# A hybrid block on one core: scan terms added by four on GpSimd, a column-split out-projection, earlier fetches of head sums

## The chip, the cores and the metric

The kernel runs on one core of a Trainium2 chip. The core has five engines with their own queues, each worked off in order: TensorE (PE in the profile, with its weight loads as PEld), VectorE (DVE), ScalarE (ACT), GpSimd (POOL) and SyncE (SP), which here only issues DMAs. The metric is device time in microseconds of one execution; smaller is better.

## The reference

The input is an image batch `x` of (4, 128, 64, 64) in float32. Layer 0 is a convolutional block with a selective scan in it, layer 1 is attention followed by a mixture of experts.

```python
# layer 0: x = x + conv_block(group_norm(x))
xn = ln(group_norm(x));  y = xn + fc2(gelu(ln(depthwise3x3(xn))))
chunks = ln(y) split into 4 groups of 32 channels          # 16 sequences of 4096 tokens
xin, z = split(chunks @ in_proj.T)                          # 64 inner channels each
xin = silu(causal_conv1d(xin, 4 taps))
dt, Bm, Cm = split(xin @ x_proj.T);  delta = softplus(dt @ dt_proj.T + b)
h_t = exp(delta_t * A) * h_{t-1} + delta_t * B_t * xin_t    # 16 states n per channel
y_t = sum over n of C_t[n] * h_t[n]  + D_skip * xin_t
m = (y * silu(z)) @ out_proj.T + skip * chunks
x = x + ln(xn + m) @ proj.T + b
# layer 1, tokens t of (4, 4096, 128)
t = t + softmax(q k^T / sqrt(128)) v @ W_proj               # 4 heads of 32
p = softmax(ln(t) @ router);  take the top 2 of 8 experts, renormalised
t = t + sum over the two of p_e * (ln(t) @ expert_e + b_e)
```

## The kernel before

All work is in one program whose order on every engine is written out by hand: each instruction is issued through a small wrapper (`queued`, line 445) that chains it to the one before it on its engine. That is why almost every instruction carries line 445 in the profile, and why one goes by the names of tiles.

An image is cut into eight blocks of 512 tokens (`BLK`), which gives 32 blocks. The scan of a block is done in two halves `p` (64 of the 128 channels each, two chunks of 32) and for 16 states `n`, so 1024 units of one scan each. A loop over `slot` does one unit per turn, and beside it one group of attention, and stages of two lanes of other tasks. One slot holds, in this order:

- the DMAs that were collected by `send` go out on SP (`flush`), and SP fetches the rows of B and C of the unit three slots ahead (tile `rows`);
- ScalarE copies the last state and computes the decay `da` of the next unit;
- a group of attention: TensorE makes scores `sc` of two key tiles for 1024 queries from `qs` and `ks`, ScalarE takes their exp (`pT`);
- the unit's scan on VectorE (`scan`): the product `h` of the B row and `du`, the scan over 512 tokens into `h`, the product `hc` of the C row and `h`;
- stages of the lanes X and Y, a generator's step at a time (`advance`);
- TensorE sums `hc` over the states into the PSUM tile `y`, by a product with the identity; the term of a unit is due some slots after its scan (`due`);
- the weighted sums `av` of the attention group of the slot before (`weighted`).

For image 0 each `hc` is a product of its own, one slot after its scan. For the other images GpSimd adds the `hc` of an odd state onto that of the even state before it, and the sum is one product two slots later. `hc` has five buffers.

Lane Y runs the norms (`first_norm`), the convolution (`conv`: on TensorE for image 0, on VectorE for the others) and `inputs`, which makes `xin`, the gate `zs`, `delta`, `du` (on GpSimd) and the rows of B and C, which go to DRAM by way of the tile `bc`. Lane X runs `closed` for a block whose two scans are done: it multiplies the gated `y` (`zs`) by `wout`, two accumulated products of 128 columns into one PSUM tile; `wout[:, p]` has values only in the 64 output columns of half `p`. It goes on to the norm, the projection and the queries, keys and values. Keys and queries are kept as a high half `hi` (rounded to fp32r) and a low half `lo`, both sent to DRAM. ScalarE copies the PSUM tile to `full` and to `hi`, and one stage later VectorE subtracts them in `lower`. Lane X also runs `divided`, once for 1024 queries, which brings the attention sums of the four heads back from DRAM (tile `avl`, two buffers), transposes them on TensorE and divides by the denominators (`rden`, `ao`); and `finished`, which applies the router and the eight experts to a block.

Each lane has one PSUM tile at a time (`ps_X`, `ps_Y`), so the next product of a lane waits until the last one has been read. Attention of an image can begin once its first quarters are closed, and after the last scan some 157 groups of attention are left.

A second program part (`any_scores`) handles inputs with too large scores; it is not entered with these inputs.

Of the kernel before, what the change touches and what calls it, by code (L numbers as in the profile page):

```python
# [9 lines left out]
F32 = mybir.dt.float32  # L10
# [26 lines left out]
def conv_mamba_attn_moe_kernel(ctx: ExitStack, tc: tile.TileContext, t: dict):  # L37
# [637 lines left out]
    def inputs(b, i, p):  # L675

        xn, pairs = xn_of[b, i], pairs_of[b, i]
        r = slice(DI * p, DI * p + DI)
        ps = work("Y")
        summed(ps, [(inxc[:, j, :], pairs[:, p, 2 * j : 2 * j + BLK]) for j in range(2)])  # L680
        pz = work("X")
        mm(pz, inz[r, :], xn[r, 3 : 3 + BLK])
        yield
        xin = mix.tile([P, BLK], F32, name="xin", bufs=2)
        scalar.activation(xin, ps, AF.Silu, bias=cb)
        zs = mix.tile([P, BLK], F32, name="zs", bufs=4)
        scalar.activation(zs, pz, AF.Silu)
        yield

        pb = work("X")  # L690
        mm(pb[0:DI, :], wbc, xin)
        ps = work("Y")
        mm(ps, wdt, xin)
        yield
        bc = mix.tile([DI, BLK], F32, name="bc")
        scalar.copy(bc, pb[0:DI, :])
        bcd = dram.tile([2, NST, 2 * BLK], F32, name="bcd", bufs=4)
        send(bcd.rearrange("c n (k q) -> (c n k) q", k=2), bc)

        e = tmp("Y", "e")  # L700
        scalar.activation(e, ps, AF.Abs, bias=dtb)
        scalar.activation(e, e, AF.Exp, scale=-1.0)
        ln = tmp("Y", "ln")
        scalar.activation(ln, e, AF.Ln, bias=1.0)
        delta = mix.tile([P, BLK], F32, name="delta", bufs=2)
        scalar.activation(delta, ps, AF.Relu, bias=dtb)
        yield
        yield

        du = mix.tile([P, BLK], F32, name="du", bufs=2)  # L710
        lost = du
        gpsimd.tensor_scalar(lost, e, 1.0, -1.0, ALU.add, ALU.add)
        gpsimd.tensor_sub(lost, e, lost)
        gpsimd.tensor_add(ln, ln, lost)
        gpsimd.tensor_add(delta, delta, ln)
        gpsimd.tensor_mul(du, delta, xin)
        in_of[b, i, p] = xin, zs, delta, du, bcd
        yield
        yield
        yield  # L720
# [18 lines left out]
    def scan(b, i, p, n, w, da):  # L739

        du = in_of[b, i, p][3]
        h = mix.tile([P, BLK], F32, name="h", bufs=3)
        vector.tensor_mul(h, w[:, 0, :], du)
        vector.tensor_tensor_scan(
            out=h, data0=da, data1=h, initial=0.0 if i == 0 else states[b % 2][:, p, n : n + 1],
            op0=ALU.mult, op1=ALU.add,
        )
        hc = mix.tile([P, BLK], F32, name="hc", bufs=5)
        vector.tensor_mul(hc, w[:, 1, :], h)
        return h, hc  # L750

# [9 lines left out]
    def closed(b, i):  # L761

        if i == 0:
            kqv[b] = [], [], [], dram.tile([P, NTILE * C], F32, name="td")
        kd, qd, vd, td = kqv[b]
        j, u = divmod(i, 2)
        if u == 0:
            kd.append(dram.tile([P, 2, 2 * BLK], F32, name=f"kd{j}"))
            qd.append(dram.tile([P, 2, 2, 2 * BLK], F32, name=f"qd{j}"))
            vd.append(dram.tile([NH, 2, P, NT * 2 * DH], F32, name=f"vd{j}"))  # L770
        kd, qd, vd, sj = kd[j], qd[j], vd[j], slice(u * BLK, (u + 1) * BLK)
        s = slice(i * BLK, (i + 1) * BLK)
        cm = tmp("X", "cm")
        vector.scalar_tensor_tensor(
            cm.rearrange(IMAGE, w=IMG), xn_of[b, i][:, 3:].rearrange(IMAGE, w=IMG), skip,
            y0_rows(b, i), ALU.mult, ALU.add,
        )
        xr = load_x(t["xtok"][b], i, "xr")
        yield
        yield  # L780
        ps = work("X")
        summed(ps, [(wout[:, p, :], gated.pop((b, i, p))) for p in range(2)])
        yield
        vector.tensor_add(cm, ps, cm)
        gpsimd.tensor_add(by_tile(xr), by_tile(xr), projb[:, None, :].to_broadcast([P, NT, C]))
        yield
        ps = transposed("X", by_tile(cm))
        yield
        xt = yield from normalised("X", by_tile(ps))
        ps = transposed("X", xt)  # L790
        yield
        f = tmp("X", "f")
        scalar.activation(f, ps, AF.Identity, bias=lnb, scale=lnw)
        yield
        ps = work("X", [P, NT, C])
        for j in range(NT):
            mm(ps[:, j, :], f[:, j * P : (j + 1) * P], projT)
        yield
        tt = side.tile([P, NT, C], F32, name="tt")
        vector.tensor_add(tt, ps, by_tile(xr))  # L800
        send(tsave[b][:, s], tt.rearrange("p j c -> p (j c)"))
        xt = yield from normalised("X", tt)

        tr = tmp("X", "tr", [P, NT, C])
        gpsimd.tensor_add(tr, tt, crow[:, None, :].to_broadcast([P, NT, C]))
        send(td[:, s], tr.rearrange("p j c -> p (j c)"))
        ps = transposed("X", xt)
        yield
        xa = tmp("X", "xa")
        scalar.copy(xa, ps)  # L810
        yield
        split = []
        for d, w, bias in ((kd, wkn, bkn), (qd, wqn, bqn)):
            ps = work("X")
            mm(ps, w, xa)
            yield
            full = side.tile([P, BLK], F32, name="full")
            scalar.activation(full, ps, AF.Identity, bias=bias)
            hi = side.tile([P, BLK], F32R, name="hi", bufs=2)
            scalar.activation(hi, ps, AF.Identity, bias=bias)  # L820
            yield

            split.append((d, full, hi))
            lower(split.pop(), sj)
        ps = work("X", [P, NT, NH, DH])
        for j in range(NT):
            mm(ps[:, j].rearrange("p h d -> p (h d)"), xa[:, j * P : (j + 1) * P], wv)
        yield
        vector.tensor_copy(vst[:, :, :, 0:DH], ps.rearrange("p j h d -> p h j d"))
        send(vd[:, u].rearrange("h p q -> p h q"), vst.rearrange("p h j d -> p h (j d)"))  # L830
        yield
        yield
        yield

    def lower(what, s):
        d, full, hi = what
        lo = side.tile([P, BLK], F32R, name="lo", bufs=2)
        vector.tensor_sub(lo, full, hi.bitcast(F32))
        for half, w in enumerate((hi, lo)):
            w = w.bitcast(F32)  # L840
            if len(d.shape) == 4:
                send(d[:, :, half, s], w[:, None, :].to_broadcast([P, 2, BLK]))
            else:
                send(d[:, half, s], w)

# [124 lines left out]
    def divided(b, q):  # L972

        ao = att.tile([P, 2, NT, NH, DH], F32, name="ao", bufs=2)
        ao_of[b, q] = ao

        def load(h):
            w = att.tile([P, BLK], F32, name="avl", bufs=2)
            sync.dma_start(out=w, in_=partial.pop((b, q, h)))
            return w  # L980

        ahead = load(0)
        yield
        yield
        for h in range(NH):
            now = ahead
            if h + 1 < NH:
                ahead = load(h + 1)
            ps = transposed("X", by_tile(now))
            yield  # L990
            ps = ps.rearrange("p (j u d) -> p u j d", u=2, d=2 * DH)
            rden = small.tile([P, 2, NT, 1], F32, name="rden")
            vector.reciprocal(rden, ps[:, :, :, DH : DH + 1])
            vector.tensor_mul(
                ao[:, :, :, h, :], ps[:, :, :, 0:DH], rden.to_broadcast([P, 2, NT, DH])
            )
            yield
# [175 lines left out]

    groups = attention_groups()
    units = [(b, i, p, n) for b, i in blocks for p in range(2) for n in range(NST)]
    rows, decays, old, due = {}, {}, None, deque()
    even, y_of, waiting, slot = None, {}, None, 0
    while slot < len(units) or due or waiting or left or lanes["X"] or running:
        flush()

# [14 lines left out]
        if slot < len(units):  # L1195
            unit = units[slot]
            h, hc = scan(*unit, rows.pop(slot), decays.pop(slot))
            old = unit, h
            b, i, p, n = unit

            if b == 0:
                due.append((slot + 1, unit, hc, n == 0))
            elif n % 2 == 0:
                even = hc
            else:
                gpsimd.tensor_add(even, even, hc)
                due.append((slot + 2, unit, even, n == 1))
        if not taken:
            advance("X", True)

# [134 lines left out]
```

## Time and profile before

| | |
|---|---|
| median of 3 runs | 5853.91 us (5849.08 to 5866.08) |
| the profiled execution | 5853.82 us, span 5852.1 us |
| granted TensorE clock, mean | 0.94 |
| PE busy | 5075.6 us (87%) |
| DVE busy | 4221.9 us (72%) |
| ACT busy | 3988.0 us (68%) |
| POOL busy | 2033.6 us (35%) |
| DMA | 1030.33 MB, mean 176 GB/s |

The span is the time from the first to the last instruction of the program. Busy time is the union of an engine's instructions. Matmuls are pipelined and their ends are modelled, so what a matmul costs is better read from the starts of it and of the next one than from its duration. "Idle before" is the time an engine stood still before an instruction, and the name after the arrow is what ended the wait. float32 products are issued as two instructions each, the fp32r scores as one.

### The profile page before, as it was taken

The numbers are of one execution on the slowest core, as the hardware profiler recorded it, in microseconds if no ns is written. First come the engines' busy times: TensorE is split into PE (matmuls) and PEld (weight loads), VectorE is DVE, ScalarE is ACT, GpSimd is POOL, SyncE is SP. The second block draws the span as 40 slices with busy tenths as digits, with TensorE's granted clock in tenths as the row PEclk, the third lists the DMA queues.
The fourth block names the chain that finished last, engine by engine and source line by source line (L and its number), as shares of the span: only waits on it lengthen the run. The fifth ranks groups of instructions, "written<-read, shape, count | busy, mean of one in ns | idle before, by whom it ended". The sixth has DMA issues, their size and how long they took to land. (4 is left out here: it accounts for less than half of the span.)

```text
span 5852.1 us, 61426 instructions
## 1 busy us (share of the span) xinstructions
PE 5075.6 (87%) x18378; PEld 2129.7 (36%) x18378; DVE 4221.9 (72%) x7155; ACT 3988.0 (68%) x6116; POOL 2033.6 (35%) x1821
## 2 busy tenths in 40 slices
PE   4676898988989898898999998898999998998896
PEld 2222343333333333333333333333333343343332
DVE  4888766778877787787888887888888888712222
ACT  3454676877767776777777776677877777665452
POOL 2333222335423443444443443444443434310000
PEclk8777999999999998999999999999999999999997
DMA  3455565556545555556555555457555555533211
GB/s 98 167 177 169 196 203 182 190 209 223 202 149 172 198 186 197 172 198 219 185 199 199 188 199 191 155 196 252 191 192 199 183 201 185 190 134 102 99 58 35
DMA packets 405509, 1030.33 MB, mean 176 GB/s; under 512 B 42785, under 2 KB 126130, under 8 KB 405170
## 3 DMA queue, kind: packets, MB, share of 16 engines
q1 hardware_dynamic: 404002, 1025.53, 51.5%
q8 instruction: 149, 2.44, 0.2%
q14 instruction: 190, 1.56, 0.1%
q10 hardware_dynamic: 1168, 0.80, 0.1%
HBM read 875.11 MB, written 134.22 MB: 172 GB/s over the span
## 5 line engine op out<-in xcount | busy, mean ns | idle before, releaser
L445 ACT ACTIVATE pT<-sc 128x1024 f32<-128x1024 f32 x2048 | 1981.1, 1020 | 879.0 <-PE sc L445 875.5
L445 PE MATMUL av<-pT,v 128*64 128x512 f32 x8192 | 2012.4, 612 | 0.5 <-ACT avs L445 0.2
L445 DVE TENSOR_TENSOR_SCAN h<-da,state,h 128x512 f32<-128x512 f32 x896 | 1271.6, 1419 | 276.2 <-ACT da L445 191.5
L445 PE MATMUL sc<-qs,ks 128*128 128x512 f32 x4096 | 1326.7, 445 | 76.7 <-ACT pT L445 40.3
L445 POOL TENSOR_TENSOR hc<-hc 128x512 f32<-128x512 f32 x384 | 557.4, 1452 | 1541.4 <-DVE hc L445 1367.3
L445 PEld LDWEIGHTS sc<-qs,ks 128*128 128x128 f32 x4096 | 724.5, 193 | 663.0 <-issue 240.9
L445 PEld LDWEIGHTS av<-pT,v 128*64 128x64 f32 x8192 | 503.9, 138 | 1198.3 <-issue 1115.1
L445 DVE TENSOR_TENSOR hc<-rows,h 128x512 f32<-128x512 f32 x1024 | 828.2, 809 | 73.6 <-DVE h L445 2.3
L445 DVE TENSOR_TENSOR h<-rows,du 128x512 f32<-128x512 f32 x1024 | 821.7, 802 | 57.3 <-DMA rows<-bcd 30.9
L445 PE MATMUL y<-hc,ident 128*128 128x512 f32 x1280 | 734.3, 660 | 79.6 <-DVE hc L445 70.0
L445 ACT ACTIVATE da<-delta,amat 128x512 f32<-128x512 f32 x1024 | 749.7, 732 | 30.9 <-DVE h L445 28.7
L445 ACT COPY state<-h 128x1 f32<-128x1 f32 x896 | 176.8, 197 | 373.3 <-DVE h L445 373.0
L445 DVE SCALAR_TENSOR_TENSOR acc<-ps_X,prX,acc 128x128 f32<-128x128 f32 x864 | 301.8, 349 | 169.6 <-PE ps_X L445 145.3
L445 ACT ACT_TABLE_LOAD x318 | 408.0, 1283 | 20.0 <-PE ps_Y L445 15.3
L445 PE MATMUL ps_X<-w_ew,xf 128*128 128x512 f32 x432 | 257.2, 679 | 112.4 <-DVE acc L445 112.2
L445 PEld LDWEIGHTS y<-hc,ident 128*128 128x128 f32 x1280 | 248.7, 206 | 257.1 <-DVE hc L445 129.6
L445 DVE RECIPROCAL rden<-ps_X 128x8 f32<-128x8 f32 x64 | 13.0, 203 | 348.8 <-PE ps_X L445 348.6
L445 POOL TENSOR_SCALAR rsX<-mvX 128x4 f32<-128x4 f32 x92 | 48.3, 525 | 600.6 <-DVE mvX L445 593.6
L445 POOL TENSOR_SCALAR du<-e 128x512 f32<-128x512 f32 x64 | 129.3, 2020 | 322.3 <-ACT e L445 322.3
L445 POOL TENSOR_TENSOR avs<-avs,prev 128x512 f32<-128x512 f32 x64 | 94.6, 1478 | 420.4 <-ACT avs L445 345.8
L445 POOL TENSOR_SCALAR rsY<-mvY 128x4 f32<-128x4 f32 x100 | 54.9, 549 | 533.6 <-DVE mvY L445 532.0
L445 ACT ACTIVATE xt<-ps_Y,shiftY,rsY 128x128 f32<-128x128 f32 x380 | 143.5, 467 | 127.4 <-POOL shiftY L445 119.9
(244 smaller groups left out, 5052.1 us busy)
## 6 DMA issues: line engine op xcount, KB each, us to landing
rows<-bcd SPq DMA_DIRECT2D x1024, 512.0 KB, 4.9
ks<-kd SPq DMA_DIRECT2D x256, 512.0 KB, 6.3
qs<-qd SPq DMA_DIRECT2D x130, 512.0 KB, 5.6
v<-vd SPq DMA_DIRECT2D x256, 256.0 KB, 6.2
avd<-avs SPq DMA_DIRECT2D x128, 256.0 KB, 2.0
pairs<-xn SPq DMA_DIRECT2D x128, 128.5 KB, 2.4
qd<-hi SPq DMA_DIRECT2D x32, 512.0 KB, 5.6
qd<-lo SPq DMA_DIRECT2D x32, 512.0 KB, 5.9
```

The costliest lines, as they stand in the source:

```text
L445: return lambda *args, **kw: queued(op(*args, **kw))
```

## The change

It has four parts, and two changes of buffers that go with them. GpSimd adds four terms `hc` of successive states into one, and TensorE multiplies only the sum of four by the identity; terms are left alone in the first half of image 0 (slots 0 to 127, `ALONE`) and no longer in its second half; `hc` has six buffers. The out-projection writes two separate products of 64 columns into the two halves of the PSUM tile. The head sums are fetched two heads ahead, with three buffers. The low half is computed by VectorE from the PSUM tile in one operation, right after `hi`, and `full` and `lower` go. The tile `bc` takes its place in the rotation of lane Y's four scratch buffers.

```diff
--- before.py
+++ after.py
@@ -692,7 +692,7 @@
         ps = work("Y")
         mm(ps, wdt, xin)
         yield
-        bc = mix.tile([DI, BLK], F32, name="bc")
+        bc = tmp("Y", "bc")[0:DI, :]
         scalar.copy(bc, pb[0:DI, :])
         bcd = dram.tile([2, NST, 2 * BLK], F32, name="bcd", bufs=4)
         send(bcd.rearrange("c n (k q) -> (c n k) q", k=2), bc)
@@ -745,7 +745,7 @@
             out=h, data0=da, data1=h, initial=0.0 if i == 0 else states[b % 2][:, p, n : n + 1],
             op0=ALU.mult, op1=ALU.add,
         )
-        hc = mix.tile([P, BLK], F32, name="hc", bufs=5)
+        hc = mix.tile([P, BLK], F32, name="hc", bufs=6)
         vector.tensor_mul(hc, w[:, 1, :], h)
         return h, hc
 
@@ -779,7 +779,9 @@
         yield
         yield
         ps = work("X")
-        summed(ps, [(wout[:, p, :], gated.pop((b, i, p))) for p in range(2)])
+        for p in range(2):
+            r = slice(DI * p, DI * p + DI)
+            mm(ps[r, :], wout[:, p, r], gated.pop((b, i, p)))
         yield
         vector.tensor_add(cm, ps, cm)
         gpsimd.tensor_add(by_tile(xr), by_tile(xr), projb[:, None, :].to_broadcast([P, NT, C]))
@@ -809,19 +811,23 @@
         xa = tmp("X", "xa")
         scalar.copy(xa, ps)
         yield
-        split = []
         for d, w, bias in ((kd, wkn, bkn), (qd, wqn, bqn)):
             ps = work("X")
             mm(ps, w, xa)
             yield
-            full = side.tile([P, BLK], F32, name="full")
-            scalar.activation(full, ps, AF.Identity, bias=bias)
             hi = side.tile([P, BLK], F32R, name="hi", bufs=2)
             scalar.activation(hi, ps, AF.Identity, bias=bias)
+            lo = side.tile([P, BLK], F32R, name="lo", bufs=2)
+            vector.scalar_tensor_tensor(
+                lo, ps, bias, hi.bitcast(F32), ALU.add, ALU.subtract
+            )
+            for half, w in enumerate((hi, lo)):
+                w = w.bitcast(F32)
+                if len(d.shape) == 4:
+                    send(d[:, :, half, sj], w[:, None, :].to_broadcast([P, 2, BLK]))
+                else:
+                    send(d[:, half, sj], w)
             yield
-
-            split.append((d, full, hi))
-            lower(split.pop(), sj)
         ps = work("X", [P, NT, NH, DH])
         for j in range(NT):
             mm(ps[:, j].rearrange("p h d -> p (h d)"), xa[:, j * P : (j + 1) * P], wv)
@@ -831,17 +837,6 @@
         yield
         yield
         yield
-
-    def lower(what, s):
-        d, full, hi = what
-        lo = side.tile([P, BLK], F32R, name="lo", bufs=2)
-        vector.tensor_sub(lo, full, hi.bitcast(F32))
-        for half, w in enumerate((hi, lo)):
-            w = w.bitcast(F32)
-            if len(d.shape) == 4:
-                send(d[:, :, half, s], w[:, None, :].to_broadcast([P, 2, BLK]))
-            else:
-                send(d[:, half, s], w)
 
 
 
@@ -975,17 +970,17 @@
         ao_of[b, q] = ao
 
         def load(h):
-            w = att.tile([P, BLK], F32, name="avl", bufs=2)
+            w = att.tile([P, BLK], F32, name="avl", bufs=3)
             sync.dma_start(out=w, in_=partial.pop((b, q, h)))
             return w
 
-        ahead = load(0)
+        ahead = deque(load(h) for h in range(2))
         yield
         yield
         for h in range(NH):
-            now = ahead
-            if h + 1 < NH:
-                ahead = load(h + 1)
+            now = ahead.popleft()
+            if h + 2 < NH:
+                ahead.append(load(h + 2))
             ps = transposed("X", by_tile(now))
             yield
             ps = ps.rearrange("p (j u d) -> p u j d", u=2, d=2 * DH)
@@ -1173,8 +1168,10 @@
 
     groups = attention_groups()
     units = [(b, i, p, n) for b, i in blocks for p in range(2) for n in range(NST)]
+
+    ALONE = NB // 2 * 2 * NST
     rows, decays, old, due = {}, {}, None, deque()
-    even, y_of, waiting, slot = None, {}, None, 0
+    four, y_of, waiting, slot = None, {}, None, 0
     while slot < len(units) or due or waiting or left or lanes["X"] or running:
         flush()
 
@@ -1198,13 +1195,14 @@
             old = unit, h
             b, i, p, n = unit
 
-            if b == 0:
+            if slot < ALONE:
                 due.append((slot + 1, unit, hc, n == 0))
-            elif n % 2 == 0:
-                even = hc
+            elif n % 4 == 0:
+                four = hc
             else:
-                gpsimd.tensor_add(even, even, hc)
-                due.append((slot + 2, unit, even, n == 1))
+                gpsimd.tensor_add(four, four, hc)
+                if n % 4 == 3:
+                    due.append((slot + 2, unit, four, n == 3))
         if not taken:
             advance("X", True)
```

## The prediction

> **What bounds the kernel now.** I read the page's first two parts first, then the busy time by stage, then the order of work inside a slot.
>
> ```profile
> PE 5075.6 (87%) x18378; PEld 2129.7 (36%) x18378; DVE 4221.9 (72%) x7155; ACT 3988.0 (68%) x6116; POOL 2033.6 (35%) x1821
> PE   4676898988989898898999998898999998998896
> PEclk8777999999999998999999999999999999999997
> ```
>
> TensorE is busy nearly throughout from slice 5 on, but 87% is a mean over stages. So I cut the span where the scans of slot 0, 128 and 256 and the last scan stand in the timeline (102, 577, 1180 and 5117 us):
>
> ```profile
> 100.00:577.00 477.00, 315.66 (x661) 119.76 (x661) 403.72 (x561) 240.69 (x470) 155.03 (x141) 0.75 0.50 170
> 577.00:1180.00 603.00, 554.86 (x1926) 228.10 (x1928) 426.23 (x607) 439.89 (x668) 166.28 (x154) 0.96 0.57 195
> 1180.00:5117.00 3937.00, 3526.59 (x13188) 1490.20 (x13183) 3196.97 (x5244) 2926.15 (x4509) 1647.54 (x1412) 0.96 0.57 194
> 5117.00:5852.00 735.00, 638.63 (x2496) 272.61 (x2493) 171.66 (x625) 357.65 (x433) 44.60 (x64) 0.93 0.25 85
> ```
>
> Columns: stage, length, busy PE, PEld, DVE, ACT, POOL with counts, granted clock, DMA. Stage 1 (slots 0 to 127) belongs to VectorE (404 of 477). Stage 2 (slots 128 to 255) is TensorE's at 92%, VectorE at 71%. Stage 3 (768 slots of 5.13 us) has TensorE at 90% and VectorE at 81%: led by one, closely followed by the other. The tail is attention alone. Two stretches of exactly eight slots show how the lead changes inside stage 3:
>
> ```profile
> 4446.57:4490.62 44.05, 43.87 (x150) 16.45 (x148) 35.42 (x72) 34.75 (x51) 13.61 (x9) 1.00 0.57 196
> 4530.50:4567.97 37.47, 35.35 (x152) 16.33 (x152) 35.72 (x53) 31.33 (x55) 17.57 (x19) 1.00 0.63 210
> ```
>
> In the first TensorE never stops. In the second VectorE leads by a hair. Cut into eights throughout, TensorE leads in 70 of stage 3's 96 stretches and VectorE in 26.
>
> **Scan terms by four.** The price on TensorE is read from starts, since its ends are modelled:
>
> ```profile
> 864.99 1.19 PE L445 MATMUL sc<-qs,ks 128*128 128x512 f32 x4
> 866.02 1.02 PE L445 MATMUL y<-hc,ident 128*128 128x512 f32 x2
> 866.97 1.94 PE L445 MATMUL av<-pT,v 128*64 128x512 f32 x8
> 868.83 1.19 PE L445 MATMUL sc<-qs,ks 128*128 128x512 f32 x4
> ```
>
> One y product is two passes and takes 0.95 us (866.02 to 866.97). Before there are 256 for image 0 and 8 for each of the other images' 48 half blocks, 640 in all (the page's 1280 passes). Afterwards there are 128 for slots 0 to 127, and a quarter of 896 slots makes 224, so 352. That is 288 fewer, 274 us of TensorE: 96 in stage 2 (91 us) and 192 in stage 3 (182 us). Stage 1 and the tail lose none.
>
> GpSimd gets 288 more additions (384 to 672). At 1.45 us that is 418 us, to 42% of the span; the engine has the room. What they do to VectorE is the real cost:
>
> ```profile
> 4009.42 2.20 POOL L445 TENSOR_TENSOR hc<-hc 128x512 f32<-128x512 f32 x1
> ```
> ```profile
> 4008.85 1.69 DVE L445 TENSOR_TENSOR_SCAN h<-da,state,h 128x512 f32<-128x512 f32 x1 [0.88 <-ACT da L445]
> 4010.64 1.52 DVE L445 TENSOR_TENSOR hc<-rows,h 128x512 f32<-128x512 f32 x1
> 4012.09 0.68 DVE L445 TENSOR_TENSOR h<-rows,du 128x512 f32<-128x512 f32 x1
> 4012.88 1.28 DVE L445 TENSOR_TENSOR_SCAN h<-da,state,h 128x512 f32<-128x512 f32 x1
> 4014.26 0.69 DVE L445 TENSOR_TENSOR hc<-rows,h 128x512 f32<-128x512 f32 x1
> ```
>
> Beside the addition a scan took 1.69 and a product 1.52 us. A slot later, with GpSimd idle, they took 1.28 and 0.69. So one addition can cost VectorE 1.24 us. It can also cost nothing: the expert sums, bn_stats and other reads of PSUM show the same time under GpSimd as without it. Over the whole trace VectorE's instructions exceed the undisturbed time of their own kind by 459 us, all of it where GpSimd runs. Shared out by overlap, 163 us fall to the 384 additions, 0.42 us each. I take 0.42, since the new additions stand in the same place of the slot, and keep 0 and 1.28 (the whole of an undisturbed addition) as ends: 122 us of VectorE, between 0 and 369.
>
> The Trainium skill, "SBUF — State Buffer", section "Who interferes with whom", speaks against the change here: a VectorE instruction with two SBUF inputs and a GpSimd one that reads SBUF exclude each other, and the later fully waits. The 0.42 us agree in which instructions suffer, but are a third of a full wait. If every addition cost a full wait, the saving of the next paragraph would be some 24 us and not 158.
>
> What reaches the end: I cut stages 2 and 3 into stretches of eight slots. In each I take 0.95 us per y off TensorE, put 0.42 us per addition on VectorE, and let the stretch shrink or grow with the larger of PE, DVE and ACT, its idle time kept. The first stretch above goes from 43.87 to about 41.7; the second loses 0.85 on VectorE, which leads. The sums, with the out-projection in them, are 54 us for stage 2 and 104 for stage 3. With stretches of four slots (the engines tied closely) they are 34 and 70, with sixteen 65 and 162. I take eight, since buffers let an engine run a slot or so ahead and no further, while slots differ in who leads. So 158, and 104 to 227 as ends.
>
> New waits. The last addition is followed by its y two slots later, as before, and y began a median 6.4 us after its addition (4.6 at the quartile), so TensorE seldom waits; attention's weighted sums and the next scores would be queued behind it. Reuse of hc's buffers goes from two slots' distance to one: the product of slot k+1 would write where y of slot k still reads. In this trace it starts a median 2.5 us after that y's end; moved to the new slots, 5 places of stage 3 would wait, 7 us together. On GpSimd the norm chains and the du chain stand behind more additions, but du is ready 14 us ahead of its first use at nine places in ten. Together I take 5 us, bounds 0 and 40.
>
> **Out-projection.** Two accumulated 128-column products (four passes, 1.42 us to the next start, and 0.4 more before the scores behind them are done) become two 64-column ones. The nearest row is attention's av, whose pairs share the array: eight passes in 1.87 us, so 0.94 for four. Some 0.9 us by 32 blocks, 28 us of TensorE, already in the sums.
>
> **Head sums.** TensorE's idle time before these transposes:
>
> ```profile
> L445 PE MATMUL ps_X<-ident,avl 128*128 128x128 f32 x256 | 47.3, 314 | 62.8 <-DMA avl<-avd 49.7 <-DVE h L445 5.5 <-PE ps_X L445 1.6
> ```
>
> A load lands in 5.7 us and had one stage. By the timeline 33 of the 63 us stand before head 0, whose load moves nowhere; 29 before heads 1 to 3. I take half, 15 us (0 to 29). VectorE's 348.6 us before rden is mostly one wait in the tail and buys nothing. One more load stands early in SP's queue ahead of a rows fetch, some 0.45 us of issue, hidden by rows being fetched three slots ahead.
>
> **Low halves.** ACT loses 64 copies of 0.70 us (45 us); it does not lead, so nothing directly. VectorE's subtraction, 0.705 us, becomes one that reads PSUM (like kinds 0.74), and stands at the same place of its queue.
>
> ```profile
> L445 DVE TENSOR_TENSOR lo<-full,hi 128x512 fp32r<-128x512 f32 x64 | 45.1, 705 | 88.2 <-ACT hi L445 88.1
> ```
>
> VectorE's 88 us of waiting for hi shrink, by 25 when I move hi 0.7 us forward at each of the 64 places. But the PSUM bank is now free only after lo: the next product, with scores and everything else of TensorE behind it, started 0.05 us after hi. Laid over the 64 places it starts 40 us later in all, 1 to 3 us where VectorE is late. I take 10 us lost (a gain of 25, a loss of 40). The bc buffer moves into a rotation of four; its copy out lands in 2.3 us, long before reuse: nothing.
>
> **The sum.** -158 +5 -15 +10 = -158 against 5853.82 us of the profiled execution (span 5852.1 and 1.7 around it; the median of the runs is 5853.91). Forecast 5696 us.
>
> **Rivals.** (a) *TensorE's relief comes through nearly whole*: sixteen-slot coupling (227), all 29 of the heads, the low halves at +25: 281, about 5575. For it: ACT idles 517 us in stage 3 before exp for scores alone, so it follows TensorE. Against: VectorE is at 81% already. (b) *GpSimd's port price makes the kernel slower.* The eight-slot sum is nil at about 1.4 us of VectorE per addition; at 1.7 it is 65 us lost, about 5919. It needs two VectorE instructions to be held fully by most additions. For it: the pair above at 1.24 us. Against: the mean of 384. At 1.28 the eight-slot sum is 24 us gained, with the rest about 5830: the edge of my range. (c) *The bank held for lo, late additions and a clock that falls oftener* take half the gain, about 5775. The granted clock stood at half in 55 stretches of stage 3, 286 us together, each after a short lull of TensorE; a third more of them would cost TensorE up to 48 us.
>
> The Trainium skill, "TensorE: Matmul & The Clock Gate", section "HAM oscillation", explains (c): idle gaps above some 3.4 us halve the clock, and a less loaded TensorE has more of them.
>
> **Chances.** Forecast 0.60; (a) 0.13; (c) 0.14; (b) 0.13, of which 0.09 is slower and 0.04 within 0.3% (18 us, about what a measurement of this kernel can tell). So faster 0.87, same 0.04, slower 0.09. The range 5575 to 5830 spans (a), the forecast and (c), and leaves out (b) and the far side of (a).
>
> **What would show it.** Right: 704 y passes, about 404 us at the present 0.574 each; stage 2 near 550 us and stage 3 near 3825; POOL near 2450; hc, h and scan means up by some 5%, PE's share of stage 3 about 87%, DVE's near 86%. Wrong: hc and h means above 1 us, DVE over 92% in stage 3, or long idle time of PE before the products that follow lo and before y.

## The result and the profile after

The changed kernel took 5934.44 us (median of 4 runs, 5926.9 to 5936.78), against 5854.53 us for the kernel before beside it: 80 us slower, ratio 1.0132 with an interval of 1.0114 to 1.015. The forecast was 5696. The profiled execution took 5926.9 us, with a span of 5925.0; the span of the kernel before was 5852.1.

The page of the kernel after, first its busy times, then TensorE and its granted clock in 40 slices, then the chain that ended last by engine:

```profile
PE 4893.2 (83%) x17802; PEld 2027.8 (34%) x17802; DVE 4411.9 (74%) x7155; ACT 3957.8 (67%) x6052; POOL 2457.8 (41%) x2109
PE   4676797878888787888888888888888888899996
PEclk7777898999999898999999999999999999999997
DVE 38%; PE 29%; ACT 13%; issue 8%; POOL 8%; DMA 4%; SPq 0%; DVEq 0%; POOLq 0%; ACTq 0%
```

TensorE did get relief: 182 us less busy. But the slices show where it went: they read 8 where they read 9 before. TensorE now stands still more often, and the chain that ended last runs through VectorE (38%) more than through TensorE (29%). The page before has no such chain; in `e2_low_only` to `e4_heads_only` below, which change the time little, TensorE has 35 to 38% of it and VectorE 30 to 34%. The stages, cut at the same events (scans of slots 128 and 256, last scan), with the columns of the prediction:

```profile
579.30:1176.20 596.90, 495.31 (x1744) 199.29 (x1744) 479.11 (x606) 437.09 (x662) 309.40 (x250) 0.91 0.57 196
1176.20:5201.40 4025.20, 3403.44 (x12797) 1419.33 (x12798) 3333.45 (x5244) 2902.72 (x4459) 1928.85 (x1605) 0.95 0.56 189
```

Stage 2 went from 603 to 597 us (forecast 54 less in the sums). Stage 3 went from 3937 to 4025, where 104 less was forecast, and this is the loss. In it TensorE is busy 123 us less and VectorE 136 us more, the stage is 88 us longer, and TensorE's time not busy rose from 410 to 622 us. The tail is 11 us shorter.

The groups that the added work touches, before and then after (columns as on the page: busy time, mean ns, then idle time before them and what ended it):

```profile
L445 POOL TENSOR_TENSOR hc<-hc 128x512 f32<-128x512 f32 x384 | 557.4, 1452 | 1541.4 <-DVE hc L445 1367.3 <-DVE rden L445 68.2 <-PE sc L445 36.0
L445 DVE TENSOR_TENSOR_SCAN h<-da,state,h 128x512 f32<-128x512 f32 x896 | 1271.6, 1419 | 276.2 <-ACT da L445 191.5 <-ACT pT L445 1.4 <-DVE h L445 1.4
L445 DVE TENSOR_TENSOR h<-rows,du 128x512 f32<-128x512 f32 x1024 | 821.7, 802 | 57.3 <-DMA rows<-bcd 30.9 <-POOL du L445 26.1
```
```profile
L445 POOL TENSOR_TENSOR hc<-hc 128x512 f32<-128x512 f32 x672 | 982.0, 1461 | 1739.7 <-DVE hc L445 1632.3 <-DVE mX L445 47.3 <-DVE rden L445 43.4
L445 DVE TENSOR_TENSOR_SCAN h<-da,state,h 128x512 f32<-128x512 f32 x896 | 1357.7, 1515 | 254.8 <-ACT da L445 168.9 <-DVE h L445 1.8 <-ACT xt L445 0.5
L445 DVE TENSOR_TENSOR h<-rows,du 128x512 f32<-128x512 f32 x1024 | 878.9, 858 | 47.7 <-POOL du L445 29.3 <-DMA rows<-bcd 18.3
L445 PE MATMUL y<-hc,ident 128*128 128x512 f32 x704 | 443.3, 720 | 119.2 <-DVE hc L445 66.6 <-POOL hc L445 52.2
```

The scans went from 1419 to 1515 ns on average and the `h` products from 802 to 858. Shared out by overlap as in the prediction, the 672 additions cost VectorE 330 us, 0.49 each. But the 384 of the kernel before cost 163 of them, so that each of the 288 new ones costs 0.58, and VectorE is busy 190 us more in all (4412 against 4222), where the prediction put 122: 136 us more for the 192 new additions of stage 3, or 0.7 each. The price of 0.42 was too low. What TensorE waits for, before and then after (us in total, times, longest):

```profile
PE ps_X L445 <- DVE acc L445: 136.5, 99, 8.3
PE ps_X L445 <- ACT xt L445: 90.8, 57, 5.1
PE sc L445 <- ACT pT L445: 40.3, 63, 4.6
PE ps_X L445 <- ACT hi L445: 24.1, 34, 2.1
PE y L445 <- POOL hc L445: 9.2, 7, 1.9
```
```profile
PE ps_X L445 <- DVE acc L445: 159.4, 96, 8.2
PE ps_X L445 <- ACT xt L445: 131.9, 71, 7.7
PE sc L445 <- ACT pT L445: 70.2, 85, 4.6
PE ps_X L445 <- DVE lo L445: 54.7, 57, 4.1
PE y L445 <- POOL hc L445: 52.2, 13, 5.4
```

Two of these come from the change: the wait for `lo`, where `hi` stood with 24.1, and the wait for the additions before `y`, which was 9.2. The first three are old waits for the other engines' steps of the lanes and for the exp, and they took up much of the time that TensorE saved.

### The profile page after: what moved, and what is told of

Its sections match the earlier page's. It is cut to its first block, busy times and chain, and to the rows that moved or that the text cites. A ratio compares the mean times of both kernels' runs of the same rounds, so it can differ in the third digit from the quotient of the medians.

```text
span 5925.0 us, 60915 instructions
## 1 busy us (share of the span) xinstructions
PE 4893.2 (83%) x17802; PEld 2027.8 (34%) x17802; DVE 4411.9 (74%) x7155; ACT 3957.8 (67%) x6052; POOL 2457.8 (41%) x2109
## 4 chain that ended last, share of the span: by engine, by line
DVE 38%; PE 29%; ACT 13%; issue 8%; POOL 8%; DMA 4%; SPq 0%; DVEq 0%; POOLq 0%; ACTq 0%
DVE h L445 19%; PE av L445 10%; PE ps_X L445 7%; DVE hc L445 6%; PE sc L445 6%; PE ps_Y L445 4%; ACT pT L445 4%; DVE cm L445 4%; DVE acc L445 3%; ACT L445 3%; ACT xt L445 2%; PE y L445 2%; POOL du L445 1%; POOL rsX L445 1%; POOL rsY L445 1%
## 5 line engine op out<-in xcount | busy, mean ns | idle before, releaser
L445 PE MATMUL av<-pT,v 128*64 128x512 f32 x8192 | 2058.3, 625 | 1.4 <-ACT avs L445 1.0
L445 POOL TENSOR_TENSOR hc<-hc 128x512 f32<-128x512 f32 x672 | 982.0, 1461 | 1739.7 <-DVE hc L445 1632.3
L445 DVE TENSOR_TENSOR_SCAN h<-da,state,h 128x512 f32<-128x512 f32 x896 | 1357.7, 1515 | 254.8 <-ACT da L445 168.9
L445 DVE TENSOR_TENSOR h<-rows,du 128x512 f32<-128x512 f32 x1024 | 878.9, 858 | 47.7 <-POOL du L445 29.3
L445 PE MATMUL y<-hc,ident 128*128 128x512 f32 x704 | 443.3, 720 | 119.2 <-DVE hc L445 66.6
L445 DVE TENSOR_TENSOR_SCAN h<-da,h 128x512 f32<-128x512 f32 x128 | 187.4, 1464 | 53.9 <-ACT da L445 42.2
L445 PEld LDWEIGHTS y<-hc,ident 128*128 128x128 f32 x704 | 144.7, 223 | 240.9 <-DVE hc L445 124.6
L445 PE MATMUL ps_X<-ident,xt 128*128 128x128 f32 x368 | 99.8, 337 | 142.8 <-ACT xt L445 131.9
```

What stands on the lines that cost most here:

```text
L445: return lambda *args, **kw: queued(op(*args, **kw))
```

## The experiments

The questions were: which of the four parts loses; if it is the additions, whether by the price on VectorE, by TensorE's new waits, or because TensorE's relief is worth less than counted; and whether the price comes from GpSimd's port or its queue. Each kernel is compared with the kernel before beside it.

**The parts alone.** `e1_four_only` is the kernel before with the sums of four and the moves of `hc` and `bc` that go with them.

> The kernel before with the additions by four alone (six hc buffers and bc in lane Y's rotation come with it). Theory one, the additions by four are the loss: the changed kernel is 80 us slower than the kernel before, so this one should be 40 to 100 us slower, with PE's idle time before y near 50 us and VectorE's busy time up by some 150 to 190 us. Theory two, the loss sits in the low halves and the product that now waits for them: this one should be 50 to 150 us faster than the kernel before, as the prediction had it.

5959.88 us, ratio 1.0167 (1.0153 to 1.0181): 102 us slower. The sums of four lose all of it and more. Its stage 3:

```profile
1168.00:5223.00 4055.00, 3450.20 (x12794) 1441.40 (x12794) 3332.02 (x5245) 2930.34 (x4507) 1933.65 (x1605) 0.94 0.56 188
```

118 us longer than before. The other three parts, each put alone into the kernel before (the hunks are those of the diff; with `e4_heads_only` goes the move of `bc`):

> The kernel before with the low halves read from PSUM in one operation, alone. Theory one (additions by four): within 20 us of the kernel before. Theory two (low halves): 60 us slower or more; in the trace of the changed kernel TensorE idles 49 us before the two products that follow lo, against 23 us before, so by that account alone it would be some 26 us slower.

> The kernel before with the out-projection as two 64-column products, alone. 28 us of TensorE go; all theories expect 10 to 28 us faster, unless the switch from 128 to 64 columns costs something.

> The kernel before with the head sums fetched two ahead (bc in lane Y's rotation comes with it, for room), alone. All theories expect 0 to 29 us faster, 15 taken.

Low halves: 5866.88, ratio 1.0011 (1.0003 to 1.002), some 6 us slower by the ratio (the medians differ by 9). Out-projection: 5854.42, ratio 0.9995 (0.9986 to 1.0003), nothing, although TensorE is busy 13 us less (5062.4 against 5075.6). Head sums: 5847.41, ratio 0.998 (0.9971 to 0.9989), some 12 us faster by the ratio (10 by the medians), within the forecast's bounds of 0 to 29. None of these explains the loss.

**Is it the wait before `y`?** In `e1_four_only`'s timeline GpSimd and then TensorE show how the sum of four can come late:

```profile
3516.74 1.28 POOL L445 TENSOR_TENSOR hc<-hc 128x512 f32<-128x512 f32 x1 [12.49 <-DVE hc L445]
3518.00 2.43 POOL L445 TENSOR_SCALAR du<-e 128x512 f32<-128x512 f32 x1
3520.51 1.60 POOL L445 TENSOR_TENSOR du<-e,du 128x512 f32<-128x512 f32 x1
...
3525.22 2.07 POOL L445 TENSOR_TENSOR du<-delta,xin 128x512 f32<-128x512 f32 x1
3527.26 1.72 POOL L445 TENSOR_TENSOR hc<-hc 128x512 f32<-128x512 f32 x1
```
```profile
3529.02 2.08 PE L445 MATMUL y<-hc,ident 128*128 128x512 f32 x2 [3.60 <-POOL hc L445]
3531.03 3.68 PE L445 MATMUL av<-pT,v 128*64 128x512 f32 x8
...
3536.97 1.94 PE L445 MATMUL av<-pT,v 128*64 128x512 f32 x8
```

The addition of the third state, which did not exist before, waits for its `hc` and starts at 3516.74; the five steps of the `du` chain stand behind it until 3527.3, and only then comes the fourth state's addition. `y` waits 3.60 us, and the next weighted sums take 3.68 instead of 1.94 us: the profile's granted clock is half from 3528.55 to 3535.38 us. `e5_later_y` is the changed kernel with the sums due one slot later, except the last of a half block. It has one more `hc` buffer, and for the room it undoes the head sums.

```diff
-        hc = mix.tile([P, BLK], F32, name="hc", bufs=6)
+        hc = mix.tile([P, BLK], F32, name="hc", bufs=7)
-                    due.append((slot + 2, unit, four, n == 3))
+                    due.append((slot + (2 if n == NST - 1 else 3), unit, four, n == 3))
```

> The changed kernel with y of a group of four due three slots after its last scan instead of two (except the group that ends a half block), hc with seven buffers, and for the room the head sums fetched one ahead as before. Theory one, lateness on GpSimd: the third addition stands behind the du chain (9 us), y waits for it with scores and weighted sums behind it, and the clock halves after each such lull. Then TensorE's idle time before y falls from some 52 us to under 10 and the kernel is 30 to 70 us faster than the changed one. Theory two, the port: VectorE's instructions are slowed by the additions wherever y stands; then within 15 us of the changed kernel, or up to 10 us slower for the head sums.

5915.43, ratio 1.0092 (1.0075 to 1.0109). TensorE's wait for GpSimd before `y`, 52.2 us in the changed kernel, is gone from the list. The stage:

```profile
1174.00:5176.00 4002.00, 3396.46 (x12798) 1420.69 (x12799) 3328.55 (x5245) 2900.89 (x4459) 1919.33 (x1605) 0.95 0.57 190
```

23 us shorter than the changed kernel's, and still 65 longer than before. VectorE is as busy as in the changed kernel (3329 against 3333 us). Undoing the head sums shows in the tail, 737 us against 724, and hardly here, for `e4_heads_only` moves stage 3 by 3 us. So the lateness is real, but it is the smaller part.

**What is TensorE's relief worth?** `e6_half_adds` is `e1_four_only` with the third state's addition left out, so that its term is missing from the sum. It has as many additions in images 1 to 3 as the kernel before, but half the `y` products.

```diff
-                gpsimd.tensor_add(four, four, hc)
+                if n % 4 != 2:
+                    gpsimd.tensor_add(four, four, hc)
```

> The additions by four alone, but the addition of the third state of each group left out, so its term is missing from the sum. y products stay at 352; additions are 448 instead of 672, in images 1 to 3 as many and in the same places as in the kernel before. Both theories (lateness and port) expect TensorE's relief to come through here: 5700 to 5800 us. A third theory, that TensorE's relief is worth little because VectorE and the lanes' chains set the pace, expects 5830 to 5860.

5820.97, ratio 0.9931 (0.9915 to 0.9948): 38 us faster by the medians. The profiled execution is 28 us faster than the one before, 18 in stage 2 and 11 in stage 3. Stage 3, and three of TensorE's waits over the whole run:

```profile
1161.00:5087.00 3926.00, 3395.98 (x12802) 1429.26 (x12802) 3208.61 (x5245) 2928.44 (x4508) 1645.92 (x1413) 0.95 0.58 194
```
```profile
PE ps_X L445 <- DVE acc L445: 162.9, 126, 8.3
PE ps_X L445 <- ACT xt L445: 115.6, 70, 7.7
PE sc L445 <- ACT pT L445: 68.0, 86, 4.6
```

This is the finding of the study. In stage 3 192 products are gone, 182 us by the prediction's price, with VectorE at 3209 us as good as unchanged. TensorE's busy time fell by 131 us; the stretches with a granted clock of one half rose from 287 to 362 us together, and half of that rise, some 38 us, is more of the 182. The stage is 11 us shorter, so 120 of the 131 became idle time, and the same old waits for `acc`, `xt` and `pT` grew as in the changed kernel, though only one `y` waited for an addition, 1.9 us.

The other direction, `e10_more_y`: the kernel before with 192 of the `y` products of images 1 to 3 issued twice (`y` is then too large).

```diff
+            if b > 0 and n % 4 == 3:
+                mm(y_of[b, i, p], ident, term, False, False)
```

> The kernel before with 192 more y products on TensorE, in images 1 to 3: the sum of every second pair is multiplied twice and so counted twice. 182 us more of TensorE, nothing else changed. If VectorE's chain sets the pace and TensorE's time is mostly cover: 10 to 60 us slower. If TensorE sets the pace, as the prediction had it: 120 to 180 us slower.

5929.73, ratio 1.0124 (1.0107 to 1.0141), and stage 3:

```profile
1185.00:5195.00 4010.00, 3658.58 (x13573) 1554.07 (x13570) 3191.03 (x5244) 2934.58 (x4509) 1636.01 (x1412) 0.97 0.56 190
```

73 us longer for the same nominal 182: 40% comes through when TensorE is loaded, against 6% when it is relieved. Every stage is read from one execution, so such shares are rough: in the six kernels `e7_more_adds` to `e12_fewer_taps`, here and below, which change nothing before slot 256, stage 2 took 604 to 606 us against 603, and if the 10 us between the two figures for `e6_half_adds` all lay in stage 3, its 6% would be 12%. The stretches at half clock fell to 222 us here, so the clock pays back a part.

**What is VectorE's time worth, and what is the price made of?** `e7_more_adds` is the kernel before (with `bc` moved, for room) and 192 more GpSimd additions in images 1 to 3, whose result nobody reads. `e8_more_adds_free` lets them read constant taps, so that they wait for nothing. `e9_more_memsets` puts 576 fills in their place, which read nothing.

```diff
+                if n % 4 == 2:
+                    junk = mix.tile([P, BLK], F32, name="junk")
+                    gpsimd.tensor_add(junk, hc, hc)        # e7
+                    gpsimd.tensor_add(junk, crow4, crow4)  # e8, crow4 = taps[:, 0:4, :]
+                    for _ in range(3):                     # e9
+                        gpsimd.memset(junk, 0.0)
```

> The kernel before (bc in lane Y's rotation for room) with one more GpSimd addition in every fourth slot of images 1 to 3, on the term of the third state, into a tile that nobody reads: 192 more additions that wait for their hc, all y products kept. Port theory: 80 to 95 us more of VectorE, 40 to 100 us slower. Lateness theory: y is due as before and only one addition stands ahead of it as before, but the du chain is late; 30 to 80 us slower with idle time of TensorE before y. Third theory: under 20 us, as TensorE leads.

> As the run with more additions, but the additional ones read a constant tile and so wait for nobody: the same 192 additions of the same size on GpSimd and the same port. Port theory: as slow as the run with more additions, within 15 us. Lateness theory: GpSimd is not held up waiting for hc ahead of the du chain, so at most half of that run's loss.

> As the run whose additional additions read a constant tile, but each of the 192 is replaced by three fills of a 128x512 tile, some 1.4 us of GpSimd that reads nothing from SBUF. Port theory (VectorE is slowed by GpSimd's reads, and its time goes straight into the span): within 20 us of the kernel before. Lateness theory (GpSimd's own chains come later): as slow as the two runs with more additions, 70 us or more.

5939.14 (ratio 1.0133, 1.0116 to 1.015), 5941.97 (the same ratio and interval) and 5867.45 (1.002, 1.0011 to 1.003). Stage 3 of `e7_more_adds` and of `e9_more_memsets`, and their scans:

```profile
1180.00:5200.00 4020.00, 3549.40 (x13184) 1493.25 (x13183) 3298.47 (x5244) 2931.09 (x4508) 1883.09 (x1604) 0.96 0.56 190
L445 DVE TENSOR_TENSOR_SCAN h<-da,state,h 128x512 f32<-128x512 f32 x896 | 1307.7, 1459 | 269.9 <-ACT da L445 184.9 <-ACT pT L445 1.8 <-ACT xt L445 0.9
```
```profile
1181.00:5132.00 3951.00, 3524.78 (x13188) 1487.45 (x13187) 3198.13 (x5245) 2928.19 (x4508) 1924.21 (x1988) 0.97 0.57 193
L445 DVE TENSOR_TENSOR_SCAN h<-da,state,h 128x512 f32<-128x512 f32 x896 | 1268.2, 1415 | 274.2 <-ACT da L445 189.6 <-ACT pT L445 1.4 <-DVE h L445 1.4
```

GpSimd is busy 236 us more in the one and 277 us more in the other, but only the additions lengthen VectorE's instructions: 3298 us against 3197 before, 0.53 us for each of the 192, while with the fills VectorE stands at 3198. In `e8_more_adds_free`, where the additions wait for nothing, stage 3 is as long:

```profile
1185.00:5205.00 4020.00, 3554.39 (x13192) 1503.37 (x13189) 3306.95 (x5245) 2928.19 (x4508) 1921.02 (x1604) 0.96 0.57 190
```

TensorE's wait for GpSimd before `y`, 9.2 us before, is 35.3 in `e7_more_adds` but 9.1 in `e8_more_adds_free`, so late sums are not what these two lose by. The price is paid through the reads of SBUF, not through GpSimd's queue. And of the 101 us that VectorE works more in `e7_more_adds`, 83 reach the end of the stage (82%), of the 110 in `e8_more_adds_free` again 83 (75%), with TensorE's products unchanged.

To see whether less VectorE time is worth as much, `e11_no_adds` leaves out the kernel before's additions but keeps the products (odd states are missing from `y`), and `e12_fewer_taps` leaves out four of the nine taps of the convolution of images 1 to 3 on VectorE. Its expectation says that taps of image 0 on TensorE go too; they stay.

```diff
-                gpsimd.tensor_add(even, even, hc)
+                pass                                       # e11
+            elif k in (1, 3, 5, 7):
+                pass                                       # e12, in the taps on VectorE
```

> The kernel before with the 384 additions of pairs left out, so that every second term is missing from the sum; y products stay. The trace of before puts 163 us of VectorE's excess on them. Port theory: 110 to 160 us faster. If TensorE sets the pace: within 30 us of the kernel before.

> The kernel before with four of the nine taps of the convolution left out, 96 instructions of 0.75 to 1.0 us on VectorE in images 1 to 3 (about 85 us; 32 tensor-engine taps of image 0 go with them, 30 us of TensorE in stages 1 and 2). Nothing of GpSimd changes. If VectorE sets the pace: 60 to 100 us faster. If TensorE does: 0 to 30 us faster.

5789.06 (0.9883, 0.9866 to 0.9899) and 5820.64 (0.9943, 0.9926 to 0.9959). Their stage 3:

```profile
1184.00:5057.00 3873.00, 3497.55 (x13184) 1479.44 (x13183) 3024.11 (x5244) 2925.18 (x4508) 1088.35 (x1029) 0.97 0.58 197
```
```profile
1185.00:5076.00 3891.00, 3497.91 (x13188) 1481.44 (x13185) 3112.67 (x5152) 2924.22 (x4508) 1644.15 (x1412) 0.97 0.58 196
```

64 us shorter for 173 us less of VectorE, and 46 for 84: 37% and 55%. `e12_fewer_taps` touches no addition, so it is VectorE's time as such that counts.

**A version that keeps the useful part.** `e13_pairs_early` is the kernel before with sums of two from slot 128 on, where image 0 had terms alone, with the head sums, the out-projection and `bc` of the change; `e14_changed_pairs` is the changed kernel with sums of two in place of four.

```diff
-            if b == 0:
+            if slot < NB // 2 * 2 * NST:
```

> The kernel before with what gained or cost nothing alone: the head sums two ahead, the out-projection in 64 columns, and pairs (not fours) also in the second half of image 0, where VectorE is at 71% of the stage. Stage 2 loses 64 y products (61 us of TensorE) and gets 64 additions; by the run with half of the additions, whose stage 2 was 18 us shorter, I expect 8 to 15 us there, 10 from the heads and 3 from the out-projection: 20 to 30 us faster than the kernel before. If the price of 0.4 us per addition held there too, 26 us would be lost in stage 2 and the kernel would come out at the kernel before's time or slower.

> The changed kernel with pairs in place of fours from slot 128 on; the other three parts stay. If the additions by four are the whole loss: 10 to 30 us faster than the kernel before. If the low halves or the buffers hold a loss that shows only beside the other parts: slower than the kernel before.

5824.52 (0.9943, 0.993 to 0.9957) and 5826.87 (0.995, 0.9936 to 0.9963) against 5855.81: some 30 us faster than the kernel before, and both beat the changed kernel by over 100 us. `e13_pairs_early` in stages 2 and 3:

```profile
581.00:1172.00 591.00, 508.04 (x1794) 206.20 (x1792) 455.35 (x606) 438.98 (x668) 261.04 (x218) 0.94 0.58 198
1172.00:5097.00 3925.00, 3509.78 (x13191) 1476.88 (x13191) 3205.16 (x5245) 2929.04 (x4509) 1652.71 (x1413) 0.96 0.57 194
```

In stage 2 VectorE had room (71%), and there pairs shorten the stage by 12 us; the head sums alone do not (`e4_heads_only` has 607 there). Of the rest, some 10 us lie in the tail, where the head sums alone gain 7, and 12 in stage 3, for which no run shows a cause. Fours instead of pairs cost 107 us between `e14_changed_pairs` and the changed kernel.

## Why the prediction was wrong

**The step that failed** is "let the stretch shrink or grow with the larger of PE, DVE and ACT, its idle time kept". It gave TensorE's relief in full wherever TensorE led, in 70 of 96 stretches, and charged VectorE only where VectorE led. The runs show in its place that stage 3 goes at the pace of both: 75 to 82% of added VectorE time comes through (`e8_more_adds_free`, `e7_more_adds`), 37 to 55% of removed, 40% of added TensorE time (`e10_more_y`) and 6% of removed (`e6_half_adds`). The idle time was not kept: TensorE's freed time turned into idle time, in waits for VectorE and ScalarE. So 0.95 us of TensorE given for 0.5 to 0.7 us of VectorE loses. The same step put 28 us of out-projection into the sums, of which nothing was found (`e3_out_only`). Neither of the other sizes of stretch mends this: four slots and sixteen both said "faster". Nor does the price of an addition alone: between the prediction's own 158 us at 0.42 and 24 us at 1.28, a price of 0.7 still gives a gain of some 114 us, an estimate by the straight line.

**The account of stage 3 for fours alone.** It is 118 us longer. VectorE is busy 135 us more (3332 against 3197); if 75 to 82% of that comes through, as in `e8_more_adds_free` and `e7_more_adds`, it is an estimated 101 to 111 us. The missing products take away 11 (`e6_half_adds`), and the late sums add 23 (`e5_later_y`, taken in the changed kernel and with a seventh buffer, so the two are not told apart). That makes 113 to 123. The effects need not add up, and `e1_four_only` has the most half-clock time of all the runs, 488 us. Why a new addition costs VectorE 0.7 us here and 0.53 to 0.57 in the two runs with 192 more stays open.

**New waits**, 5 us with bounds of 0 and 40: about 23, inside the bounds but mis-sized. The prediction moved `y` and the buffers forward but not GpSimd's queue: it asked whether `du` was ready in time, not what the `du` chain does to an addition that now stands behind it.

**The price of an addition**, 0.42 us, was too low: 0.53 in `e7_more_adds`, 0.57 in `e8_more_adds_free`, 0.58 by overlap for the new additions of the changed kernel and 0.7 by VectorE's whole time in its stage 3. 190 us against 122 lie inside the bounds of 0 and 369, but the new additions cost more than the old ones, where the prediction took them for equal. The Trainium skill, "SBUF — State Buffer", section "Who interferes with whom", says that a VectorE instruction with two SBUF inputs contends with a GpSimd one that reads SBUF, and not with one that only writes it. `e7_more_adds` and `e9_more_memsets` agree on both halves; on the average an addition cost VectorE 0.5 to 0.7 us, not its own undisturbed 1.28.

**Low halves**, 10 us lost: 6 to 9 alone. The bank held for `lo` is there (35.6 us of waits in `e2_low_only` and 54.7 in the changed kernel, where `hi` had 24.1) and mostly covered. **Head sums**, 15 us gained: 10 to 12. Both sizes were nearly right.

**Stage 2**: 54 gained in the sums, 6 measured, and 18 in `e6_half_adds`, where the products fell by the same 96 at two thirds of the new additions. Here too the relief passed only in part, although TensorE stood at 92%, and its half-clock time rose from 47 us to 107 in the changed kernel and 94 in `e6_half_adds`.

**The rivals.** (b) had the sign and nearly the number (5919), but not the condition: it wanted 1.4 to 1.7 us per addition, and 0.5 to 0.7 was enough, because the relief on the other side of the sum was hardly there. That its number came near is luck. The mechanisms of (c) are real, late additions and half-clock stretches (84 of them and 416 us in stage 3 of the changed kernel, 55 and 287 before), but (c) took them off a gain that did not exist. The 3.4 us that the prediction cites with (c) do not fit as a limit for one lull: in the 7 us ahead of 38 of the 55 stretches before, TensorE's longest lull was shorter by the profile's modelled ends, and the median over all 55 was 2.5 us. The tests named under "what would show it" were of little use: 704 `y` passes and POOL's 2458 us came as foretold, `hc` and `h` stayed under 1 us and VectorE at 83%, and yet the kernel lost. One sign of being wrong did come, TensorE's idle time before `y` (52.2 us) and before the products that follow `lo` (54.7). The others tested the prices; none asked whether the rest of TensorE's idle time stays as it was.

## What to carry to other kernels

Where two engines stand at 80 to 90% and hand work back and forth, the busier one need not be the bound: before trading work between them, add a known amount to each and take a known amount away, and read what share comes through. Work for GpSimd that reads SBUF was charged to VectorE here, 0.5 to 0.7 us for an addition of 1.28, so it belongs where VectorE has room, here stage 2 but not stage 3. And when an instruction is put into an in-order queue, look at what is queued between it and the next one that somebody waits for.

## What was unexpected of the hardware

Taking matmuls away lowered the granted clock: time at half clock in stage 3 rose from 287 us to 362 where little but the products changed (`e6_half_adds`), and to 416 (changed) and 488 (`e1_four_only`) where additions came with it. It fell to 222 with more products (`e10_more_y`). VectorE's load moves it too, without any change of products: 331 with more additions (`e7_more_adds`), 232 without any (`e11_no_adds`). So a part of TensorE's relief is lost to its own clock. The lull of 3.60 us in the timeline shown is one of the longer ones that go before such a stretch. GpSimd fills of 128x512 (527 ns each, 304 us in all) cost VectorE nothing and the kernel some 11 us, while 192 additions cost 80.
